# A convolution and GRU network on one core: first-image statistics on 128 partitions, matrices in long rows, a work tile less

## The chip, the cores and the metric

The kernel runs on one core of a Trainium2 chip. The metric is the device time of one execution, in microseconds (us). The median of three timed runs of the kernel before is 5883.06 us, the lowest 5861.34 and the highest 5891.94. One more execution was profiled; its own time is 5869.95 us.

## The reference, cut to what matters

The input x is (4, 64, 256, 256) in float32: four images of 64 channels. Two residual layers follow each other, each ahead of a group norm over 32 groups of two channels.

```python
x = x + conv(gn(x), w1, w_dw, w_out, ln_w, ln_b)
x = x + gru(gn(x), w_ih, w_hh, b_ih, b_hh)
```

The first layer takes the 64 channels to 384 by w1, runs a 3x3 depthwise convolution, and splits the result into q, k and v. It convolves q and k circularly in patches of 8x8 (through their Fourier transforms), normalizes over the channels, multiplies by v, and projects back to 64 channels by w_out. The second layer runs a GRU over the 256 columns of the image, in which each pixel sees three neighbours of the column before.

The group norm needs the mean and variance of every pair of channels over a whole image before the first pixel of that image can be normalized.

## The kernel before

Images are stored with their columns first, as x[b, c, w, h]. The work has three stages.

**Set-up.** A depthwise convolution followed by a Fourier transform of a patch is one linear map of a 10x10 halo (100 numbers) per channel. TensorE builds these maps from the taps (tile bt) and the depthwise weights (wd), ScalarE copies them into the tile ts (100 partitions, 384 channels, 64 numbers), and three stores on GpSimd's queue (POOL) write ts to the DRAM tensor t_all, one each for q, k and v (lines 229 to 248). Meanwhile SP's queue loads the first image in eight tiles xc (lines 249 to 255), each of 128 partitions by 4096 numbers. Partitions 0 to 63 hold the 64 channels of 16 columns in the left half of the image, 64 to 127 those of 16 columns in the right half. So there are two loads per tile, each of 64 rows of 16 KB. VectorE takes the statistics with bn_stats (512 numbers at a time) and bn_aggr. `norm_of_pieces` then joins partitions with a matmul by avg2 and gives a scale and shift per partition, sc0. Three tiles xc are held (bufs=3). After the set-up its pools are closed, and the pools of the next stage, xp for the image tiles xq among them, take their place in SBUF. Then the GRU's weights are loaded on ScalarE's queue (lines 258 to 266).

**Convolution, 32 blocks.** A block n is 32 rows of an image, in 128 patches. The loop from line 624 runs, for each block:

- pointwise, three times (chunks 0, 1, 2), 16 units each: TensorE multiplies the halos in the four tiles xq by w1, and ScalarE or VectorE copies the result from PSUM to the tile h;
- transform: 16 matrices of 100x1024 numbers for q and k and eight for v (function values) are fetched from t_all by SP into the tiles t (bufs=4, fetched four ahead, lines 329 to 340), and TensorE multiplies h by them;
- circular, twice (a = 0 and 1): the four products of the transforms of q and k (functions products and inverse);
- layer_norm, spread over the block by the generator norm, and, within the next block, gate, project and the store of the result (finish, lines 608 to 617).

The PSUM ring has eight banks. Temporary tiles q, k, pr, y, xr and others share one pool of seven work tiles of 128x1024 numbers (wk, line 278). All instructions keep the program's order on their engine (class InOrder), so a DMA that waits for a tile holds up what stands behind it on the same queue.

While the blocks of image b run, the statistics of image b+1 are taken (lines 597 to 606): look loads a quarter of a piece, four columns for each half, in two DMAs on POOL's queue into a work tile; count runs two bn_stats over it. Four quarters make a piece and eight pieces an image, so 24 of the 32 blocks do this. The work tile seen0 is held through circular(n, 0), another, seen1, from there to circular(n, 1). At an image's end norm_of_pieces runs between the pointwise units.

**GRU, 256 columns.** It reads the stored x1 column by column. Its first pools follow at line 701.

In the profile nearly all instructions have line 157, the helper that keeps the order, so they are told apart by the names of their tiles.

Of the kernel before, what the change touches and what calls it, by code (L numbers as in the profile page):

```python
# [10 lines left out]
F32 = mybir.dt.float32  # L11
AF = mybir.ActivationFunctionType
ALU = mybir.AluOpType
# [6 lines left out]
P = 128  # L20
# [63 lines left out]
def norm_of_pieces(nc, st, t, psum, eps, sc):  # L84

    m_all, d, total, mean = t[:, 128:136], t[:, 136:144], t[:, 144:145], t[:, 145:146]
    nc.vector.tensor_copy(m_all, st[:, :, 0])
    nc.vector.tensor_reduce(total, m_all, mybir.AxisListType.X, ALU.add)  # L90
    yield
    pm = psum()
    nc.tensor.matmul(pm, lhsT=t[:, 0:P], rhs=total, start=True, stop=True)
    nc.vector.tensor_copy(mean, pm)
    nc.vector.tensor_tensor(d, m_all, mean.to_broadcast([P, 8]), ALU.subtract)
    nc.vector.tensor_tensor(d, d, d, ALU.mult)
    nc.vector.tensor_tensor(d, d, st[:, :, 1], ALU.add)
    nc.vector.tensor_reduce(total, d, mybir.AxisListType.X, ALU.add)
    yield
    pv = psum()  # L100
    nc.tensor.matmul(pv, lhsT=t[:, 0:P], rhs=total, start=True, stop=True)
    nc.scalar.activation(sc[:, 1:2], pv, AF.Sqrt, bias=eps, scale=1.0)
    nc.vector.reciprocal(sc[:, 1:2], sc[:, 1:2])
    nc.vector.scalar_tensor_tensor(sc[:, 0:1], mean, -1.0, sc[:, 1:2], ALU.mult, ALU.mult)
    yield
# [57 lines left out]
def tile_conv_then_gru(  # L163
# [13 lines left out]
    bias: bass.AP,  # L177
    avg2: bass.AP,
    out: bass.AP,
):  # L180
# [6 lines left out]

    t_all = dram.tile([3, 8, HALO, 16 * NS], F32, tag="t_all", name="t_all")


    ident = const.tile([P, P], F32, tag="ident", name="ident")
    make_identity(tc.nc, ident)
    hh_sb = const.tile([P, P], F32, tag="hh", name="hh_sb")
    nc.scalar.dma_start(hh_sb, hh)
    eps = const.tile([P, 1], F32, tag="eps", name="eps")
    nc.gpsimd.memset(eps, EPS)
    w1_sb = const.tile([P, HID], F32, tag="w1", name="w1_sb")
    nc.scalar.dma_start(w1_sb, w1.rearrange("a c o -> (a c) o"))
    g_sb = const.tile([P, 2, 2, NS], F32, tag="g", name="g_sb")
    nc.scalar.dma_start(g_sb, g12.rearrange("a s r n p -> (a s) r n p"))  # L200
    wo_sb = const.tile([P, 2, C], F32, tag="wo", name="wo_sb")
    nc.scalar.dma_start(wo_sb, w_out.rearrange("a f t c -> (a f) t c"))
    ln_sb = const.tile([P, 2, 2], F32, tag="ln", name="ln_sb")
    nc.scalar.dma_start(ln_sb, ln.rearrange("a f n t -> (a f) n t"))

    def piece(of, b, i, w, n):

        for half in range(2):
            w0 = half * (W // 2) + i * (W // 16) + w
            yield slice(half * C, (half + 1) * C), of[b, :, w0 : w0 + n, :].rearrange("c w h -> c (w h)")  # L210

# [4 lines left out]
    bn0 = const.tile([P, 8, 6], F32, tag="bn0", name="bn0")  # L216
    with tc.tile_pool(name="xa", bufs=3) as xa, tc.tile_pool(name="sta", bufs=1) as sta, tc.tile_pool(
        name="bps", bufs=1, space=PSUM
    ) as bps:
        bt = sta.tile([P, 32, HALO], F32, tag="bt", name="bt")  # L220
        wd = sta.tile([P, HID], F32, tag="wd", name="wd")
        for i in range(4):
            nc.scalar.dma_start(bt[32 * i : 32 * i + 9], taps[i])
            nc.sync.dma_start(wd[32 * i : 32 * i + 9], w_dw)
        avg4 = sta.tile([P, 1024], F32, tag="avg4", name="avg4_0")
        nc.sync.dma_start(avg4[:, 0:P], avg2)
        ts = sta.tile([HALO, 3 * P, NS], F32, tag="ts", name="ts")
        banks = bps.tile([P, 8, 512], F32, tag="b", name="psb")
        for i in range(32):
            kind, s = i // 16, i % 16  # L230
# [12 lines left out]
            nc.scalar.copy(ts[:, c0 : c0 + num, 4 * s : 4 * s + 4], ps.rearrange("p s c -> p c s"))  # L243
        for i in range(3):
            nc.gpsimd.dma_start(
                t_all[i].rearrange("n p k -> p n k"),
                ts[:, i * P : (i + 1) * P].rearrange("p (n c) k -> p n (c k)", n=8),
            )
        for i in range(8):
            xc = xa.tile([P, 4096], F32, tag="xc", name=f"xc_{i}")  # L250
            for at, of in piece(x, 0, i, 0, 16):
                nc.sync.dma_start(xc[at], of)
            for k in range(8):
                nc.vector.bn_stats(bn0[:, k, :], xc[:, 512 * k : 512 * k + 512])
            nc.vector.bn_aggr(st0[:, i, :], bn0)
        for _ in norm_of_pieces(nc, st0, avg4, lambda: banks[:, 0, 0:1], eps, sc0[:, 0]):
            pass
    wi = const.tile([P, 9, C], F32, tag="wi", name="wi")
    wh = const.tile([P, 3, C], F32, tag="wh", name="wh")
    for a in range(2):  # L260
        at = slice(a * C, (a + 1) * C)
        for g in range(3):
            nc.scalar.dma_start(wi[at, 3 * g : 3 * g + 3, :], w_ih[g].rearrange("t c o -> c t o"))
            nc.scalar.dma_start(wh[at, g, :], w_hh[g])
    bias_sb = const.tile([P, 6], F32, tag="bias", name="bias_sb")
    nc.scalar.dma_start(bias_sb, bias.rearrange("a o n -> (a o) n"))
    b_rz = const.tile([P, 2], F32, tag="b_rz", name="b_rz")
# [3 lines left out]


    st1 = const.tile([P, NBLK, 2], F32, tag="st1", name="st1")
    with ExitStack() as s:
        big = s.enter_context(tc.tile_pool(name="big", bufs=1))
        xp = s.enter_context(tc.tile_pool(name="xp", bufs=4))
        tp = s.enter_context(tc.tile_pool(name="tp", bufs=4))
# [11 lines left out]
        def work(name, shape=(P, 1024)):  # L289
            return wk.tile(list(shape), F32, tag="wk", name=name)  # L290
# [3 lines left out]
        v = big.tile([P, NP, NS], F32, tag="v", name="v")  # L294
        xq = {}

        def load(n, jq):

            t = xp.tile([P, 16, HALO], F32, tag="xq", name=f"xq_{n}_{jq}")
            nc.gpsimd.dma_start(t, xh[n, :, 16 * jq : 16 * jq + 16, :])  # L300
            xq[n, jq] = t

        def normalize(n, jq):
# [25 lines left out]
        def fetch(count):  # L329
            while len(streamed) < min(count, NBLK * 24):  # L330
                m, r = divmod(len(streamed), 24)
                t = tp.tile([P, 16, NS], F32, tag="t", name=f"t_{m}_{r}")
                nc.sync.dma_start(t[0:HALO].rearrange("p c k -> p (c k)"), t_all[order[r][0], order[r][1]])
                streamed.append(t)
                matrices[m, order[r]] = t
# [122 lines left out]
        def layer_norm(n):  # L458

            st = big.tile([P, 2, NP // 2, 6], F32, tag="lnst", name=f"lnst_{n}")  # L460

# [134 lines left out]

        def look(n, k, t):

            for at, of in piece(x, n // 8 + 1, n % 8, 4 * k, 4):
                nc.gpsimd.dma_start(t[at], of)  # L600

        def count(n, k, t):
            for i in range(2):
                nc.vector.bn_stats(bn0[:, 2 * k + i, :], t[:, 512 * i : 512 * i + 512])
            if k == 3:
                nc.vector.bn_aggr(st0[:, n % 8, :], bn0)

# [11 lines left out]
        for jq in range(4):  # L619
            load(0, jq)  # L620
        for jq in range(4):
            normalize(0, jq)
        norm = None
        for n in range(NBLK + 1):
# [4 lines left out]
            if n == NBLK:  # L629
                for _ in norm:  # L630
                    pass
            if n:
                finish(n - 1)
            if n == NBLK:
                flush()
                later.pop()()
                break
            more = n // 8 + 1 < B
            if more:
                seen = work(f"seen0_{n}")  # L640
                look(n, 0, seen)
            circular(n, 0, lambda sp: count(n, 0, seen) if more and sp == 1 else None)
            if more:
                seen = work(f"seen1_{n}")
                look(n, 1, seen)
            for unit in range(16):
                pointwise(n, 1, unit, unit in (5, 8, 11, 14))
                if more and unit in (8, 14):
                    count(n, unit // 7, seen)
                    look(n, unit // 7 + 1, seen)  # L650
            flush()
            norm = layer_norm(n)

            def beside(sp):
                next(norm)
                if more and sp == 1:
                    count(n, 3, seen)

            circular(n, 1, beside)
            image = None  # L660
            if more and n % 8 == 7:
                t = work(f"avg4_{n}")
                nc.gpsimd.dma_start(t[:, 0:P], avg2)
                image = norm_of_pieces(nc, st0, t, lambda: psum()[:, 0, 0:1], eps, sc0[:, n // 8 + 1])
            for unit in range(16):
# [261 lines left out]
```

## Time and profile before

| what | value |
|---|---|
| median of three runs | 5883.06 us |
| the profiled execution | 5869.95 us |
| its span | 5868.2 us |
| TensorE (PE) busy | 5479.9 us, 93% |
| VectorE (DVE) busy | 4080.5 us, 70% |
| ScalarE (ACT) busy | 3475.4 us, 59% |
| GpSimd (POOL) busy | 500.8 us, 9% |
| moved by DMA | 818.04 MB, 139 GB/s on average |

The page cuts the span into 40 slices and gives each engine's busy share of a slice in tenths. It then follows the chain of work that ended last, lists the costliest groups of instructions with the idle time ahead of them, and the DMA queues: q0 holds the DMAs that POOL issues, q1 those of SP, q10 those of ScalarE. Other views give the instructions in order of time, the waits of an engine with what ended them, and the queues in any stretch. A busy TensorE is modelled from the records, and some records of matmuls may be missing.

### The profile page before, as it was taken

To read this page: it belongs to the slowest core of one execution; us is meant where nothing else is said; L and a number is where in the kernel's file an instruction comes from. 1 tells how busy PE (TensorE), PEld (TensorE's weight loads), DVE (VectorE), ACT (ScalarE), POOL (GpSimd) and SP (SyncE) were. 2 spreads that over 40 slices of the span, in tenths; PEclk is the share of its full clock that TensorE was granted. 3 is DMA by queue.
4 is the path that set the end of the run, shared out by engine and by line. 5 is a ranking of instruction groups with operands and counts; after the bars stand their busy time and mean duration, and the time that the engine had idled before them with its cause. 6 is when DMAs were issued, how large, how long until landed. Compare 5 with 4: busy or idle time off the path is not lost. (4 is left out here: it accounts for less than half of the span.)

```text
span 5868.2 us, 278629 instructions
## 1 busy us (share of the span) xinstructions
PE 5479.9 (93%) x127196; PEld 4762.6 (81%) x127196; DVE 4080.5 (70%) x9593; ACT 3475.4 (59%) x4604; POOL 500.8 (9%) x797
## 2 busy tenths in 40 slices
PE   2999999999999999999999999999979999999998
PEld 1878888888788878887888888878868888888888
DVE  2776777777767777777677767766667777776766
ACT  2556566665565656655655666556556666666655
POOL 0000000000000000000000000000002122222222
PEclk9999999999999999999999999999989999999999
DMA  8455555555555555555555454544444444444443
GB/s 225 135 156 147 151 151 155 154 142 152 157 147 154 150 151 159 141 150 159 150 152 150 140 143 126 142 139 125 137 114 116 116 116 117 115 117 113 116 114 81
DMA packets 561916, 818.04 MB, mean 139 GB/s; under 512 B 41353, under 2 KB 435373, under 8 KB 559677
## 3 DMA queue, kind: packets, MB, share of 16 engines
q1 hardware_dynamic: 520152, 633.59, 40.0%
q0 software_dynamic: 37776, 165.24, 9.5%
q8 instruction: 996, 16.32, 1.2%
q10 hardware_dynamic: 2808, 1.38, 0.1%
q14 instruction: 184, 1.50, 0.1%
HBM read 622.46 MB, written 144.05 MB: 131 GB/s over the span
## 5 line engine op out<-in xcount | busy, mean ns | idle before, releaser
L157 PEld LDWEIGHTS psring<-h,t 100*32 100x32 f32 x40960 | 1334.1, 115 | 294.0 <-issue 175.2
L157 PE MATMUL psring<-h,t 100*32 100x128 f32 x40960 | 1445.2, 274 | 105.9 <-issue 37.7
L157 PE MATMUL psring<-w_sb,xq 64*100 64x128 f32 x24576 | 1403.2, 271 | 55.7 <-POOL xq L157 40.2
L157 PEld LDWEIGHTS psring<-w_sb,xq 64*100 64x100 f32 x24576 | 1357.6, 164 | 117.0 <-issue 50.2
L157 ACT COPY h<-psring 100x1024 f32<-100x1024 f32 x1274 | 1205.5, 1027 | 161.4 <-PE psring L157 155.2
L157 DVE TENSOR_TENSOR pr<-psring,q 128x512 f32<-128x512 f32 (+1 forms) x576 | 463.3, 857 | 308.8 <-PE psring L157 234.8
L157 DVE BATCH_NORM_STATS2 lnst<-z 128x6 f32<-128x64 f32 x4096 | 545.4, 214 | 117.6 <-ACT z L157 117.6
L157 DVE TENSOR_TENSOR z<-z,lnm 128x1024 f32<-128x1024 f32 x512 | 612.7, 1218 | 8.8
L157 ACT COPY q<-psring 128x1024 f32<-128x1024 f32 x256 | 259.3, 1013 | 596.8 <-PE psring L157 358.9
L157 ACT ACTIVATE z<-pshz,b_rz 128x288 f32<-128x288 f32 (+7 forms) x510 | 242.6, 476 | 519.8 <-PE pshz L157 519.7
L157 PE MATMUL pshr<-st,wi 64*64 64x144 f32 (+7 forms) x12240 | 510.5, 270 | 34.9 <-issue 20.9
L157 PE MATMUL psni<-st,wi 64*64 64x144 f32 (+7 forms) x12240 | 510.4, 270 | 24.4 <-issue 22.4
L157 PE MATMUL pshz<-st,wi 64*64 64x144 f32 (+7 forms) x12240 | 510.8, 270 | 23.1 <-issue 21.9
L157 ACT COPY z<-psring 128x2048 f32<-128x2048 f32 x128 | 238.9, 1867 | 446.7 <-PE psring L157 441.7
L157 PE MATMUL psring<-pr,g_sb 32*64 32x512 f32 x8192 | 494.8, 594 | 5.7 <-issue 5.5
L157 ACT ACTIVATE y<-psring,ln_sb 128x512 f32<-128x512 f32 x512 | 372.5, 781 | 200.5 <-PE psring L157 197.0
L157 PEld LDWEIGHTS psni<-st,wi 64*64 64x64 f32 x12240 | 446.5, 133 | 45.5 <-issue 34.4
L157 PEld LDWEIGHTS pshr<-st,wi 64*64 64x64 f32 x12240 | 422.3, 133 | 52.3 <-issue 49.5
L157 DVE COPY h<-psring 100x1024 f32<-100x1024 f32 x262 | 320.3, 1223 | 198.7 <-PE psring L157 194.7
L157 PEld LDWEIGHTS pshz<-st,wi 64*64 64x64 f32 x12240 | 424.9, 133 | 37.3 <-issue 36.4
L157 DVE SCALAR_TENSOR_TENSOR g<-z,xn 128x288 f32<-128x288 f32 (+7 forms) x510 | 218.4, 428 | 311.9 <-ACT z L157 310.0
L157 POOL TENSOR_TENSOR raw<-raw,st 128x512 f32<-128x512 f32 x256 | 303.7, 1186 | 1146.0 <-ACT xn L157 548.1
(98 smaller groups left out, 7377.9 us busy)
## 6 DMA issues: line engine op xcount, KB each, us to landing
t<-t_all SPq DMA_DIRECT2D x768, 400.0 KB
xq<-in_xh POOLq DMA_DIRECT2D x128, 800.0 KB, 4.6
xr<-in_x SPq DMA_DIRECT2D x256, 256.0 KB
x<-xr SPq DMA_DIRECT2D x256, 256.0 KB
seen<-in_x POOLq DMA_DIRECT2D x192, 256.0 KB, 4.1
raw<-x SPq DMA_DIRECT2D x128, 256.0 KB
raw<-x SPq DMA_DIRECT2D x256, 128.0 KB
xt<-xn SPq DMA_DIRECT2D x256, 128.0 KB
```

The costliest lines, as they stand in the source:

```text
L157: return self.tc.keep_in_program_order(got(*args, **kwargs))
```

## The change

The change has six parts.

1. The first image's pieces have other partitions. Partition 2c + a holds channel c in half a of the image, for `(c a)` is one axis of equal steps in memory. So a piece is one DMA over 128 partitions. A tile xc is now half a piece (eight columns, rows of 8 KB), and five are held instead of three, 16 in all.
2. `norm_of_pieces` goes with it. The means of both layouts are needed (one to take from the statistics, one for the scale of xq, whose partitions are a C + c), so there are two small matrices, `sums`, and two matmuls for the mean.
3. The pool xp is opened ahead of the set-up's pools. The four loads of xq for block 0 are issued on POOL right behind the three stores of ts.
4. t_all is laid out as [3, 100, 8, 1024] instead of [3, 8, 100, 1024]. A store of one partition of ts is 32 KB in one run. A matrix is then read as 100 rows of 4 KB whose starts are 32 KB apart. The first two stores are issued after the first half of the copies.
5. The constants and the GRU's weights move to SP, between the sixth and seventh xc. The taps and wd come first on ScalarE's queue.
6. The statistics of other images use the tile lnst of the layer norm, while the layer norm doesn't, as a place for two columns at a time, and one work tile for four columns at a time. Each DMA spans 128 partitions. seen0 is gone: in circular(n, 0) no work tile is held for statistics.

```diff
 def norm_of_pieces(nc, st, t, psum, eps, sc):
...
-    nc.tensor.matmul(pm, lhsT=t[:, 0:P], rhs=total, start=True, stop=True)
+    for i in range(2):
+        nc.tensor.matmul(pm[:, i : i + 1], lhsT=t[:, P * i : P * i + P], rhs=total, start=True, stop=True)
...
-    t_all = dram.tile([3, 8, HALO, 16 * NS], F32, tag="t_all", name="t_all")
+    t_all = dram.tile([3, HALO, 8, 16 * NS], F32, tag="t_all", name="t_all")
+    layer0 = ExitStack()
+    xp = layer0.enter_context(tc.tile_pool(name="xp", bufs=4))
...
     def piece(of, b, i, w, n):
-        for half in range(2):
-            w0 = half * (W // 2) + i * (W // 16) + w
-            yield slice(half * C, (half + 1) * C), of[b, :, w0 : w0 + n, :].rearrange("c w h -> c (w h)")
+        w0 = i * (W // 16) + w
+        return of[b].rearrange("c (a w) h -> (c a) w h", a=2)[:, w0 : w0 + n, :].rearrange("p w h -> p (w h)")
...
         for i in range(4):
+            nc.scalar.dma_start(wd[32 * i : 32 * i + 9], w_dw)
             nc.scalar.dma_start(bt[32 * i : 32 * i + 9], taps[i])
-            nc.sync.dma_start(wd[32 * i : 32 * i + 9], w_dw)
...
+        def keep_matrices(i):
+            nc.gpsimd.dma_start(
+                t_all[i].rearrange("p n k -> p (n k)"),
+                ts[:, i * P : (i + 1) * P].rearrange("p c k -> p (c k)"),
+            )
...
-        for i in range(3):
-            nc.gpsimd.dma_start(
-                t_all[i].rearrange("n p k -> p n k"),
-                ts[:, i * P : (i + 1) * P].rearrange("p (n c) k -> p n (c k)", n=8),
-            )
-        for i in range(8):
-            xc = xa.tile([P, 4096], F32, tag="xc", name=f"xc_{i}")
-            for at, of in piece(x, 0, i, 0, 16):
-                nc.sync.dma_start(xc[at], of)
-            for k in range(8):
-                nc.vector.bn_stats(bn0[:, k, :], xc[:, 512 * k : 512 * k + 512])
-            nc.vector.bn_aggr(st0[:, i, :], bn0)
+            if i == 15:
+                keep_matrices(0)
+                keep_matrices(1)
+        keep_matrices(2)
+        for jq in range(4):
+            load(0, jq)
+        def seen_piece(i):
+            xc = xa.tile([P, 2048], F32, tag="xc", name=f"xc_{i}")
+            nc.sync.dma_start(xc, piece(x, 0, i // 2, i % 2 * 8, 8))
+            for k in range(4):
+                nc.vector.bn_stats(bn0[:, i % 2 * 4 + k, :], xc[:, 512 * k : 512 * k + 512])
+            if i % 2:
+                nc.vector.bn_aggr(st0[:, i // 2, :], bn0)
+        for i in range(6):
+            seen_piece(i)
...
+        for i in range(6, 16):
+            seen_piece(i)
...
-                nc.sync.dma_start(t[0:HALO].rearrange("p c k -> p (c k)"), t_all[order[r][0], order[r][1]])
+                nc.sync.dma_start(t[0:HALO].rearrange("p c k -> p (c k)"), t_all[order[r][0], :, order[r][1]])
...
+        seen = lnst.rearrange("p a i k -> p (a i k)")[:, 0:512]
-        def look(n, k, t):
-            for at, of in piece(x, n // 8 + 1, n % 8, 4 * k, 4):
-                nc.gpsimd.dma_start(t[at], of)
+        def look(n, w, t):
+            nc.gpsimd.dma_start(t, piece(x, n // 8 + 1, n % 8, w, t.shape[1] // H))
...
+            def beside_first(sp):
+                if more and sp in (0, 3):
+                    count(n, 2 * (sp // 3), seen)
+                    look(n, 2 * (sp // 3) + 2, seen)
+            circular(n, 0, beside_first)
             if more:
-                seen = work(f"seen0_{n}")
-                look(n, 0, seen)
-            circular(n, 0, lambda sp: count(n, 0, seen) if more and sp == 1 else None)
-            if more:
-                seen = work(f"seen1_{n}")
-                look(n, 1, seen)
+                four = work(f"seen_{n}")
+                look(n, 8, four)
             for unit in range(16):
                 pointwise(n, 1, unit, unit in (5, 8, 11, 14))
-                if more and unit in (8, 14):
-                    count(n, unit // 7, seen)
-                    look(n, unit // 7 + 1, seen)
+                if more and unit == 8:
+                    count(n, 4, seen)
+                    look(n, 6, seen)
+                    count(n, 8, four)
+                    look(n, 12, four)
+            if more:
+                count(n, 6, seen)
```

In place of the first `...` after `seen_piece(i)` the loads of sums, hh, w1, g, w_out, ln, w_ih, w_hh and the biases stand on SP. The first look of a block, `look(n, 0, seen)`, stands ahead of finish(n - 1). The last count, `count(n, 12, four)` with the bn_aggr, stays at sp == 1 of circular(n, 1).

## The prediction

> **What bounds the kernel now.** I read the 40 slices first. Each is 147 us long.
>
> ```profile
> PE   2999999999999999999999999999979999999998
> DMA  8455555555555555555555454544444444444443
> GB/s 225 135 156 147 151 151 155 154 142 152 157 147 154 150 151 159 141 150 159 150 152 150 140 143 126 142 139 125 137 114 116 116 116 117 115 117 113 116 114 81
> ```
>
> TensorE is full in every slice but the first, where it is busy for two tenths and the DMA engines for eight. So the kernel is bound by TensorE, except in a start-up of about one slice, and that start-up is bound by transfers. Next the timeline of the first 160 us. Its columns are start, duration, engine, line, operation, what it writes and reads, and in brackets the idle time before it and what ended that.
>
> ```profile
> 44.58 2.25 POOL L157 DMA_DIRECT2D t_all<-ts  x2 [43.22 <-ACT ts L157]
> ...
> 92.19 4.85 DVE L157 BATCH_NORM_STATS2 bn<-xc 128x6 f32<-128x512 f32 x8 [4.77 <-DMA xc<-in_x]
> ...
> 102.01 0.16 DVE L157 SCALAR_TENSOR_TENSOR sc<-avg,sc 128x1 f32<-128x1 f32 x1
> ...
> 126.77 6.07 SPq L157 DMA_DIRECT2D t<-t_all  x4
> 127.57 2.17 POOL L157 DMA_DIRECT2D xq<-in_xh  x4 [70.28 <-DMA t<-t_all]
> ...
> 136.08 1.72 ACT L157 ACTIVATE xq<-xq,sc 128x1600 f32<-128x1600 f32 x1 [34.30 <-DMA xq<-in_xh]
> ...
> 138.31 6.03 PEld L157 LDWEIGHTS psring<-w_sb,xq 64*100 64x100 f32 x64 [38.26 <-POOL xq L157]
> ...
> 147.00 1.11 DVE L157 TENSOR_SCALAR xq<-xq,sc 128x1600 f32<-128x1600 f32 x1 [13.89 <-DMA xq<-in_xh]
> ```
>
> The reader is to see a chain with idle time in it. The image's scale is ready at 102.01, yet the first image tile xq is only requested at 127.57. It waits for the matrices to land in t_all (126.77), because its pool lies where the set-up tiles were. The last of the four xq lands at 147.0, and the first pointwise stage ends at 161.3. The wait that ends last is t_all's landing, then xq's own 19.4 us.
>
> Third, the DMA queues in stretches of the start-up (packets, MB, share of 16 engines). From 28 to 42 us the loads xc are alone:
>
> ```profile
> q1 hardware_dynamic: 232, 3.01, 100.5%
> ```
>
> From 60 to 80 us xc (q1) and the stores to t_all (q0) share the engines:
>
> ```profile
> q1 hardware_dynamic: 320, 4.18, 82.8%
> q0 software_dynamic: 323, 0.82, 18.4%
> ```
>
> From 103 to 126 us t_all is the only large transfer:
>
> ```profile
> q0 software_dynamic: 1311, 3.77, 51.3%
> ```
>
> Alone, xc fills all engines and moves only 3.01 MB / 14 us = 215 GB/s, which is 13.4 GB/s per busy engine. Beside it the stores crawl at 0.82 / 20 us = 41 GB/s. Each xc row is 16 KB long and each t_all row 4 KB, so a fair turn per row would give about this split. Per busy engine, t_all does 3.77 MB / (0.513 x 16 x 23 us) = 20.0 GB/s. The xq loads, which span 128 partitions, do 20.6 late in the run (3500 to 4200 us: 17.07 MB at 7.4%). So what is slow is xc, in 64-partition halves, and what it starves.
>
> **The change, part by part.**
>
> *Start-up transfers.* Bytes hardly change. Before the last xq has landed the changed kernel moves 16.8 MB of xc, 9.8 MB of t_all, 3.3 MB of xq and about 1.5 MB of weights, taps and small matrices: 31.4 MB. I sum them as engine time at the rates above. xc in 128-partition pieces is not in this trace. Its ends are 13.4 GB/s per engine (nothing gained, 78 us) and the peak that the engines show when t_all drains (some 365 GB/s over the first 3 us from 90 us on, 46 us). I take 20.5, the rate of xq, its nearest row (128 partitions, 6.4 KB rows): 16.8 MB / (16 x 20.5) = 51 us. t_all at 20 GB/s per engine is 31 us. But its 100 rows don't load the engines evenly: by itself it took from about 85 us, with some 8.1 MB left, to 126.8, which is 194 GB/s or 51 us for all of it. Other loads now fill the gaps, so I take 36. xq at 20.6 is 10 us, the small ones 5, and the first request is out at 2.5 us. Sum: 2.5 + 51 + 36 + 10 + 5 = 104 us for the last xq, against 147.0. That is **43 us**.
>
> This needs the engines busy throughout. xq now has a pool of its own and is queued on POOL straight behind t_all, so no landing is waited for between them. The taps are issued first on ACT's queue instead of fifth to ninth (the last was issued at 12.8 us and its products began at 24.9), so t_all's first two stores should come at about 34 us instead of 44.6. By then VectorE isn't the limit: 64 statistics at 4.85/8 = 0.61 us are 39 us in all, 2.6 us per MB-piece, and the pieces come every 3.2 us. Five buffers of 1 MB cover its lag.
>
> What is late next: xq waits in the queue behind all of t_all, and the h tile lies on the set-up's tiles, so the first eviction still waits for t_all. Should the long t_all rows now take most turns from xc, the scale comes last instead of xq; the bytes are the same, the scale's own chain (97.1 to 102.0, 4.9 us) comes on top, and xq no longer trickles in. I keep both within the same number.
>
> *Weights.* Thirteen issues on ACT between 100.3 and 127.7 go. They lay beside t_all's landing and cost nothing; nor does their going give anything by itself. On SP, nine loads now stand between the sixth and the seventh xc. Each is under 0.3 MB; they are in the 5 us. If one had to wait for a tap load's landing, five pieces are already in flight to cover it.
>
> *One more matmul per image scale* (two columns for the mean): four images, 0.3 us each. 1 us.
>
> *Other images' statistics.* The order on TensorE and ScalarE stays; VectorE keeps its eight statistics per block in other places. The first layer-norm product of blocks 0, 24 and 31 starts at 238.47, 3371.24 and 4278.97. Blocks with statistics take 3132.8/24 = 130.53 us, those without 907.7/7 = 129.68. All the looking-ahead costs 0.85 x 24 = 20 us. Three image ends of 3 us each (the scale's chain, which stays) leave 11 us. In them are waits that show in VectorE's list from 160 to 3360 us (total, times, longest):
>
> ```profile
> DVE pr L157 <- DMA x<-xr: 68.4, 23, 3.8
> DVE bn L157 <- DMA seen<-in_x: 22.2, 24, 2.1
> ```
>
> From 3500 to 4300 us, without statistics, neither appears. The first is a shortage of work tiles in the first circular stage, where one tile less is now held; the second a load requested six units ahead of its use, now seven. VectorE's waits are mostly hidden behind TensorE, so of 11 us I take 4 as won. The ends are 11 won and 10 lost (each block adds a VectorE statistic ahead of the last projection; 0.4 us of it uncovered in 24 blocks).
>
> *Matrices in long rows.* Stores get longer runs; each matrix load now reads 100 rows of 4 KB that lie 32 KB apart, no longer one block. Not in this trace. Lower end: nothing, as the GRU's raw loads run well with 1 KB rows 256 KB apart (4600 to 5700 us: 122.2 MB at 40.2% of 16 engines, 17.3 GB/s each). Upper end below, as the rival. I take 0.
>
> The sum: 43 - 1 + 4 = 46 us. Against the profiled execution (5869.95 us, span 5868.2 and 1.75 around it) that is 5824. The median of the three timed runs, 5883, is 13 us above that execution, and the lowest 9 below it, so I put the forecast at **5826 us**.
>
> **Where a rule speaks against it.** xc halves show 215 GB/s with rows that start 256 KB apart; the new pieces start 128 KB apart. The Trainium skill ("DMA: Bandwidth & Descriptors", Latency and other measured facts) lists a row pitch of large powers of two as slow, 207 GB/s at 512 KiB. By it xc might stay at 207 GB/s: 81 us instead of 51, and 30 of the 46 us would go. Its page "SBUF — State Buffer" (The DMA port swizzle) gives the other reading: 64 partitions reach half of the 16 ports, at most 218 GB/s. By that one xc would be freed, at up to 436 GB/s, and the sum would be some 60 us. The raw loads above, at 17.3 per engine with the same 256 KB pitch, side with the ports, but not in a sustained stream.
>
> **The rivals.**
> *Slow rows stay slow (0.15).* xc keeps 13.4 GB/s per engine. Then xc ends near 88 us, t_all drains as before to about 124, and only the request and the gap between t_all and xq go: last xq 10 us later at 134, 13 us won instead of 43, so 5856. For it: this trace has no sustained stream of rows so far apart that is fast. Against: xq and raw.
> *Engines at their peak (0.15).* 31.4 MB at 365 GB/s is 86 us, last xq at 89, 58 us won: 5811.
> *Slower: matrix loads by far rows (0.05).* In the values stage TensorE takes a matrix of 0.41 MB each 1.86 to 1.97 us (two in the 3.71 us at 238.89), with four fetched ahead. That needs 210 to 220 GB/s. If far rows fall to half the 20 GB/s per engine, a matrix takes 2.56 us, 0.65 too long for the four not fetched ahead: 2.6 us per block, 83 in 32 blocks, so 5826 + 83 = 5909. It outweighs the gain from 46/32 = 1.4 us per block on, that is when a matrix takes over 2.27 us (180 GB/s). Against: the rows keep their 4 KB, and today TensorE waits for matrices only 9.6 us in all of 160 to 3360 us.
> *It does not do what it says:* xq might still wait for t_all through its pool; but its pool is now opened before the set-up's, so I give that nothing of its own.
>
> **How the numbers follow.** The forecast (40 to 50 us won) has 0.65, the rivals 0.15, 0.15 and 0.05. A measurement of this kernel can tell 0.5%, 29 us. Faster by more: forecast and peak, less 0.03 for noise, 0.77. Within: slow rows and that noise, 0.18. Slower by more: 0.05. The range runs from the peak with all 11 us of the steady part and from the lowest of the three runs (5811 - 7 - 9 = 5795) to the slow rows with 6 us of the possible loss in the blocks (5862).
>
> **What would show it.** A first slice with more TensorE, first pointwise at 92 to 100 us; xc alone at 300 GB/s or more; t_all landed before 100 us; the block period with statistics near 130.3; TensorE's wait for t unchanged. The forecast is wrong if xc alone stays near 215 GB/s, if t_all or the scale lands after 115 us, or if the period of the last blocks rises.

## The result, and the profile after

Five runs of the changed kernel have a median of 5838.45 us (5813.94 to 5845.49), five of the kernel before 5875.22 (5861.34 to 5891.94). The ratio is 0.9919, with a 95% interval of 0.9898 to 0.9939: about 48 us won, between 36 and 60. The profiled execution's span is 5836.7 us, 31.5 below that of before. A second group of runs gave 0.9904 [0.9880, 0.9928].

The forecast was 46 us won, at 5826 us; both stand close to this. The views must say whether it came the way that was told. First the 40 slices of the changed kernel:

```profile
PE   4999999999999999999999999999979999999998
DMA  7555555555555555555555554544444444444443
```

TensorE has four tenths of the first slice where it had two; the other slices are as they were. Then its timeline of the first 130 us (start, duration, engine, line, operation, what it writes and reads, count, and in brackets the idle time ahead and what ended it):

```profile
11.99 0.28 ACTq L158 DMA_DIRECT2D bt<-in_taps  x1
...
28.46 0.43 SPq L158 DMA_DIRECT2D bias_sb<-in_bias  x1
28.99 23.44 SPq L158 DMA_DIRECT2D xc<-in_x  x10
...
40.51 1.28 POOL L158 DMA_DIRECT2D t_all<-ts  x2 [39.17 <-ACT ts L158]
...
95.31 2.47 DVE L158 BATCH_NORM_STATS2 bn<-xc 128x6 f32<-128x512 f32 x4 [1.92 <-DMA xc<-in_x]
...
103.26 0.16 DVE L158 SCALAR_TENSOR_TENSOR sc<-avg,sc 128x1 f32<-128x1 f32 x1
...
103.55 26.03 SPq L158 DMA_DIRECT2D t<-t_all  x7
...
105.68 16.74 PE L158 MATMUL psring<-w_sb,xq 64*100 64x128 f32 x256 [4.30 <-POOL xq L158]
```

The first pointwise stage begins at 105.7 instead of 138.3, and its 256 matmuls now run in one piece to 122.4 instead of 161.3. But what came last has changed. In the trace t_all's last row ends at 86.1 us, where it ended at 125.4 before, and xq's last at 98.8. The scale is ready only at 103.26, no earlier than before: the last xc piece was counted at 97.8. The first read of t_all, at 103.55, had not waited for t_all either but for the scale, for its tile takes the place of set-up tiles. SP's list of waits from 0 to 110 us (total, times, longest) has it:

```profile
SPq L158 <- DVE sc L158: 43.2, 1, 43.2
```

The queues in three stretches show why the scale is late (packets, MB, share of 16 engines). From 35 to 40 us, xc alone:

```profile
q1 hardware_dynamic: 287, 2.10, 99.9%
```

That is 2.10 MB / 5 us = 420 GB/s, 26 per engine. From 5 to 20 us, xc beside the taps (q10):

```profile
q1 hardware_dynamic: 417, 3.04, 86.1%
q10 hardware_dynamic: 125, 0.50, 16.1%
```

The engines are as full, yet xc moves only 203 GB/s. From 60 to 78 us, xc beside the stores to t_all (q0):

```profile
q0 software_dynamic: 238, 5.32, 76.7%
q1 hardware_dynamic: 191, 1.40, 18.4%
```

Now it is xc that starves, at 78 GB/s, beside 296 on POOL's queue (275 of t_all, 21 of xq, which starts there at 57.8). The rows are 8 KB against mostly 32 KB, and the bytes stand at 1 to 3.8. Counted in rows, 171 stand against 209: again about one row of each in turn.

By position, in us of the two traces:

| | before | after | won |
|---|---|---|---|
| end of the first pointwise stage | 161.3 | 122.4 | 38.9 |
| first layer-norm product, block 0 | 238.5 | 202.2 | 36.3 |
| the 24 blocks with statistics | 3132.8 | 3139.6 | -6.8 |
| the 7 blocks without | 907.7 | 906.6 | 1.1 |
| the rest | 1589.2 | 1588.3 | 0.9 |

So the start-up holds the gain of the profiled execution. Whether the 24 blocks gained or lost can't be read from one pair of traces, as the experiments show.

### The profile page after: what moved, and what is told of

Same layout as the page of the kernel before. It is cut to its first block, busy times and chain, and to the rows that moved or that the text cites. A ratio compares the mean times of both kernels' runs of the same rounds, so it can differ in the third digit from the quotient of the medians.

```text
span 5836.7 us, 278467 instructions
## 1 busy us (share of the span) xinstructions
PE 5472.7 (94%) x127204; PEld 4752.8 (81%) x127204; DVE 4076.5 (70%) x9593; ACT 3475.0 (60%) x4604; POOL 476.3 (8%) x749
## 5 line engine op out<-in xcount | busy, mean ns | idle before, releaser
L158 DVE TENSOR_TENSOR y<-psring,y 128x1024 f32<-128x1024 f32 x256 | 312.4, 1221 | 128.8 <-ACT y L158 127.9
```

The lines of the kernel that those rows point to most:

```text
L158: return self.tc.keep_in_program_order(got(*args, **kwargs))
```

## The experiments

All kernels below compute the whole reference. Groups of runs differ in absolute time (the kernel before has medians from 5850 to 5915 us), so each is given as a ratio to the kernel before in its own group, and places in the start-up are read from its trace.

**The first image in halves again.** The theory: what freed xc is that one load spans 128 partitions. The rival: the shorter rows, or their smaller distance. Only the loads are halved; row length and distance stay.

```
-            nc.sync.dma_start(xc, piece(x, 0, i // 2, i % 2 * 8, 8))
+            for g in range(2):
+                at = slice(g * C, (g + 1) * C)
+                nc.sync.dma_start(xc[at], piece(x, 0, i // 2, i % 2 * 8, 8)[at])
```

> The changed kernel, but each piece xc of the first image comes in two loads, of partitions 0 to 63 and 64 to 127; rows of 8 KB and their distance of 128 KB stay. Theory (a load over half the partitions is slow, over all of them fast): xc alone falls from 420 GB/s (35 to 40 us of the changed kernel) to about 215, the scale is ready 25 to 35 us later than at 103.4, first pointwise at 128 to 140 instead of 105.7, and the time rises by 20 to 32 us. Rival (the shorter rows, or their smaller distance, made xc fast): xc alone stays above 380 GB/s and the time is within 6 us of the changed kernel.

Measured: 0.9959 [0.9945, 0.9973], so about half of the gain is gone. Its queues from 20 to 28 us, and its timeline:

```profile
q1 hardware_dynamic: 222, 1.44, 94.9%
q10 hardware_dynamic: 18, 0.12, 8.2%
```

```profile
131.82 0.16 DVE L158 SCALAR_TENSOR_TENSOR sc<-avg,sc 128x1 f32<-128x1 f32 x1
...
134.25 16.12 PE L158 MATMUL psring<-w_sb,xq 64*100 64x128 f32 x256 [4.30 <-POOL xq L158]
```

The engines are full and xc moves 1.44 MB / 8 us = 180 GB/s beside the last of the taps, and 1.65 MB / 8 us = 206 from 42 to 50 us without them; the scale comes 28.6 us later than in the changed kernel, and the first pointwise stage starts where the theory had it. The rival falls: the rows are the same. This settles the two readings weighed in the prediction. The Trainium skill ("SBUF — State Buffer", The DMA port swizzle and "Can I just issue two DMAs to hit both halves?") says that 64 partitions reach half of the ports, and that two transfers are not joined to fill them. Here both halves were requested one behind the other, and stayed slow. The pitch of 128 KB, in both kernels, cost the 128-partition loads nothing that shows: 420 GB/s.

**t_all in short rows again.** The theory: the 32 KB rows win their turns from xc and make the scale last.

```
-    t_all = dram.tile([3, HALO, 8, 16 * NS], F32, tag="t_all", name="t_all")
+    t_all = dram.tile([3, 8, HALO, 16 * NS], F32, tag="t_all", name="t_all")
```

(Store and fetch follow the old layout.)

> The changed kernel with the matrices stored as before: t_all is [3, 8, 100, 1024] again, rows of 4 KB. Theory (the two queues take turns row by row, so the 32 KB rows held xc back to 72 to 85 GB/s while t_all moved 264 to 333; the bytes are the bound): xc gets 200 GB/s or more beside t_all, the scale is ready at 80 to 92 us instead of 103.4, t_all lands later than 80 and xq last, first pointwise at 92 to 103 instead of 105.7; the time is 2 to 12 us lower. Rival (the long rows are what made the stores fast): t_all lands after 110, first pointwise after 115, the time rises by 8 us or more. The blocks without statistics keep 129.5 us in both.

Measured: 0.9921 [0.9898, 0.9943]. Its queues from 46 to 54 us and from 66 to 90, and its timeline:

```profile
q1 hardware_dynamic: 354, 2.57, 76.6%
q0 software_dynamic: 358, 0.77, 24.7%
...
q0 software_dynamic: 2361, 6.17, 93.6%
```

```profile
71.41 0.16 DVE L158 SCALAR_TENSOR_TENSOR sc<-avg,sc 128x1 f32<-128x1 f32 x1
...
104.79 1.47 SPq L158 DMA_DIRECT2D t<-t_all  x4
...
109.02 5.84 PE L158 MATMUL psring<-w_sb,xq 64*100 64x128 f32 x64 [39.48 <-POOL xq L158]
```

The turns change sides with the rows: 321 GB/s for xc, 96 for t_all. The scale is ready 32 us sooner, but this buys nothing: t_all's last row ends at 104.4 instead of 86.1, and xq trickles in until 117.0. Both expectations failed in part. From 66 to 90 us POOL's queue has the engines to itself and moves 257 GB/s, 224 of it t_all in 4 KB rows and the rest the first of xq. The long rows are worth 8.4 us in the start-up (first layer-norm product at 210.6 against 202.2, or 11.3 against the 199.3 of a second trace of the changed kernel), which the timed ratio doesn't resolve. In the blocks they do nothing either way: the 7 late blocks take 903.4 us here and 906.6 there, and TensorE's wait for t is 15.8 us in both from 160 to 3360 us.

**The other images' statistics as before**, in an otherwise changed kernel: old looks in halves, two work tiles.

```
-            circular(n, 0, beside_first)
+                seen = work(f"seen0_{n}")
+                look(n, 0, seen)
+            circular(n, 0, lambda sp: count(n, 0, seen) if more and sp == 1 else None)
...
+                seen = work(f"seen1_{n}")
+                look(n, 1, seen)
```

> The changed kernel with the statistics of the other images as before: halves of 64 partitions, two work tiles, four looks per block, and the old one-matmul scale for images 1 to 3. Theory (the new looks are worth nothing measurable): blocks with statistics take 130.5 to 130.9 us as in both kernels, the time is within 8 us of the changed kernel. Rival 1, as forecast (the new looks save 4 us): it is 2 to 11 us slower than the changed kernel, and the waits of VectorE for the store of xr and for seen return (68 and 22 us). Rival 2 (the new looks cost the 0.28 us per block that the two traces show): 5 to 10 us faster.

**Only the first image in 128-partition pieces**, in an otherwise unchanged kernel.

```
-        for i in range(8):
-            xc = xa.tile([P, 4096], F32, tag="xc", name=f"xc_{i}")
-            for at, of in piece(x, 0, i, 0, 16):
-                nc.sync.dma_start(xc[at], of)
...
+        for i in range(16):
+            xc = xa.tile([P, 2048], F32, tag="xc", name=f"xc_{i}")
+            w0 = i * (W // 32)
+            nc.sync.dma_start(
+                xc,
+                x[0]
+                .rearrange("c (a w) h -> (c a) w h", a=2)[:, w0 : w0 + 8, :]
...
```

> The kernel before with one part of the change alone: the first image in 16 pieces over 128 partitions (five tiles, two small matrices for its scale). Theory (pieces and early xq each carry a part): xc is through by 55 to 65 us, t_all then drains at 200 to 270 GB/s and lands at 92 to 105 instead of 126.8, the first xq is requested there, first pointwise at 104 to 117 instead of 138.3; 20 to 34 us faster than before. Rival (the gain came from the early request of xq): t_all lands after 115 and the gain is under 12 us.

**Only the early request of xq**, in an otherwise unchanged kernel: its pool is opened ahead of the set-up's, and the four loads stand behind the stores.

```
+    xp = layer0.enter_context(tc.tile_pool(name="xp", bufs=4))
...
+        for jq in range(4):
+            load(0, jq)
         for i in range(8):
```

> The kernel before with another part alone: the pool xp opened ahead of the set-up, the four xq of block 0 queued behind the stores to t_all; halves of 16 KB rows, matrices of 4 KB rows, the old statistics. Theory (the pieces carry most, the early request the rest): the stores still land near 124 to 128 us, the last xq at 130 to 138 instead of 147, first layer-norm product at 222 to 232 instead of 238.5; 8 to 16 us faster than before. Rival (the early request carries most): first layer-norm product before 215.

**Only the new looks**, in an otherwise unchanged kernel.

```
-                seen = work(f"seen0_{n}")
-                look(n, 0, seen)
...
+            circular(n, 0, beside_first)
...
+                four = work(f"seen_{n}")
+                look(n, 8, four)
```

> The kernel before with the third part alone: the other images' statistics through lnst and one work tile, over 128 partitions. The start-up stays (first layer-norm product at 238 us). Block time of the 24 blocks with statistics so far: new looks 3139.6, 3133.7, 3127.3, 3141.6 and 3127.6 us, old looks 3132.8, 3149.6, 3140.9 and 3132.1, means 3134 and 3139. Theory (worth 4 us, as forecast, below what a run can tell): 3126 to 3142 us, ratio to the kernel before 0.998 to 1.0005. Rival 1 (worth 15 us or more, which the timed medians of the run with the old looks suggest): ratio below 0.9975. Rival 2 (a cost): above 1.0005.

Measured, with the changed kernel's two groups for comparison:

| | ratio [95%] | scale ready | first pointwise stage | first layer-norm product | 24 blocks |
|---|---|---|---|---|---|
| changed kernel | 0.9919 [0.9898, 0.9939] | 103.3 | 105.7 to 122.4 | 202.2 | 3139.6 |
| changed kernel again | 0.9904 [0.9880, 0.9928] | 102.9 | 105.4 to 121.9 | 199.3 | 3141.6 |
| old looks | 0.9952 [0.9937, 0.9967] | 104.1 | 106.5 to 123.0 | 203.8 | 3149.6 |
| only the pieces | 0.9936 [0.9911, 0.9961] | 68.1 | 117.2 to 134.0 | 211.7 | 3140.9 |
| only early xq | 0.9982 [0.9966, 0.9998] | 101.0 | 139.2 to 157.8 | 234.9 | 3132.1 |
| only the new looks | 0.9981 [0.9967, 0.9994] | 101.2 | 142.6 to 165.2 | 241.8 | 3125.8 |

The pieces are the bulk: 26.8 of the 36.3 us in the start-up. Their first pointwise stage came just later than expected, since t_all landed only at about 105. The early request by itself wins 3.6 there, less than its expectation had: with slow halves, t_all still lands at 131.0 and xq at 143.3. Those 3.6 us are hardly more than what two traces of one kernel differ by (202.2 and 199.3), and the timed ratio leaves 1 to 20 us. The new looks alone win 0.0019 x 5850 = 11 us (4 to 19). Their rival of a cost falls; that of 15 us or more (below 0.9975) does not, for the interval reaches 0.9967. Taken out of the changed kernel they cost 0.0033 to 0.0048, 19 to 28 us, though across groups. That is over each range in that run's expectation, though the intervals of the two kernels just meet (0.9937 and 0.9939 at their ends); what it got right is that the two waits of VectorE return. In its trace the 7 blocks without statistics are slower too (917.7 us, 906.6 and 904.6 in the changed kernel), so not all of the difference need be the looks. VectorE's list of waits shows which went. Old looks in the changed kernel, 160 to 3360 us (total, times, longest):

```profile
DVE pr L182 <- DMA x<-xr: 60.6, 24, 3.6
DVE bn L182 <- DMA seen<-in_x: 24.0, 25, 2.0
```

The new looks in the changed kernel:

```profile
DVE pr L158 <- DMA x<-xr: 6.9, 14, 0.9
DVE bn L158 <- DMA seen<-in_x: 0.3, 1, 0.3
```

The shortage of work tiles is gone, and with it ScalarE's wait for pr (205.2 us in 41 times with the old looks, 14.0 in 7 with the new). If 191 us fewer of it are worth some 11, most of it must have lain beside TensorE's work; no run tries that by itself. The sums over 24 blocks can't settle so small a gain: kernels with new looks have 3122 to 3150 us (3160 with the 16 KB rows below), with old ones 3132 to 3150.

**The taps in 128 partitions.** Theory: the nine-partition tap loads halve xc in the first 20 us, and SP then stands at small matrices until 28.46. So the taps come padded in one load each, and the constants stand behind the 13th piece.

```
-            nc.scalar.dma_start(wd[32 * i : 32 * i + 9], w_dw)
-            nc.scalar.dma_start(bt[32 * i : 32 * i + 9], taps[i])
+        nc.scalar.dma_start(wd, w_dw)
+        nc.scalar.dma_start(bt, taps)
...
-        for i in range(6):
+        for i in range(13):
             seen_piece(i)
```

> The changed kernel, but the taps and the depthwise weights come in one load each over 128 partitions (23 rows of zeros behind each 9, 1.8 MB instead of 0.5), and the nine constants stand on SP behind the thirteenth piece xc instead of the sixth. Theory (the taps' loads over 9 partitions slow xc and, through the constants' turns on SP, hold back its issue, so xc gets 175 to 233 GB/s in the first 20 us): xc plus taps get 330 GB/s or more from 5 to 20 us, the first stores to t_all are issued at 24 to 30 instead of 40.5, first pointwise at 90 to 98 instead of 105.7, 6 to 14 us faster than the changed kernel. Rival (the start is bound by all the bytes at the rate they have): first pointwise at 104 or later, no gain.

Measured: 0.9923 [0.9903, 0.9943]; scale at 101.7, first pointwise at 104.1, not at 90 to 98. Its DMA from 15 to 30 us, and SP's timeline:

```profile
q1 hardware_dynamic: 862, 6.28, 101.1%
```

```profile
31.44 0.43 SPq L158 DMA_DIRECT2D avg<-in_sums  x1
...
72.30 0.33 SPq L158 DMA_DIRECT2D bias_sb<-in_bias  x1
77.47 5.13 SPq L158 DMA_DIRECT2D xc<-in_x  x3
```

The theory held for the first 30 us (419 GB/s; the stores went out at 32 us, a little behind the 24 to 30 expected), and the gain was lost behind them: the constants, in rows of at most 2.3 KB, took their turns against 32 KB rows, SP needed 41 us to issue nine of them, and the last three pieces waited behind.

**The same, with even rows of 16 KB for both** (store and fetch follow the layout).

```
-    t_all = dram.tile([3, HALO, 8, 16 * NS], F32, tag="t_all", name="t_all")
+    t_all = dram.tile([3, 2, HALO, 4, 16 * NS], F32, tag="t_all", name="t_all")
...
+            xc = xa.tile([P, 4096], F32, tag="xc", name=f"xc_{i}")
...
```

> The kernel of the run with taps on 128 partitions, and rows of 16 KB on both queues: pieces xc of 16 columns (three tiles), t_all as [3, 2, 100, 4, 1024]. Theory (turns go row by row, so equal rows share evenly): beside t_all xc gets 130 to 210 GB/s, the scale is ready before the last xq has landed, at 70 to 88 us, and first pointwise starts with the first xq at 84 to 95; 0 to 8 us faster than that run. Rival (the stores need their 32 KB rows to be fast): t_all lands 8 us or more later than in that run and nothing is gained.

Measured: 0.9973 [0.9959, 0.9986]. From 60 to 80 us the two queues moved the same, 185 GB/s each, within the 130 to 210 expected:

```profile
q0 software_dynamic: 465, 3.70, 53.2%
q1 hardware_dynamic: 302, 3.69, 43.6%
```

So the even turns came, but not the gain. The constants held up the scale again (102.9): the last rows of the last two of them moved only at 61 and 70 us, behind t_all's. And t_all's last row ended at 96.4, where it ended at 74.7 in the run before, as the rival had it. The kernel lost most in the blocks: 3160.3 us for 24, with TensorE waiting for t for 34.5 us in 51 times. Why this layout does so was not tried further.

**The padded taps, constants behind the sixth piece** (the lines are set against the first kernel with padded taps).

```
-        for i in range(13):
+        for i in range(6):
             seen_piece(i)
```

> The kernel with taps on 128 partitions, but the nine constants back behind the sixth piece xc, ahead of the stores to t_all. In the run with them behind the thirteenth they were issued from 31.4 us and the next xc only at 77.5: theory, that each of their rows of 0.5 to 2.3 KB waits a turn of a 32 KB row. Then here the constants are through before the stores begin (32 us), the last xc is issued before 50, the scale is ready at 84 to 95 instead of 102 to 103, first pointwise at 86 to 97; 6 to 16 us faster than the changed kernel. Rival (some other wait held back the last three xc): the scale stays above 100.

Measured: 0.9914 [0.9898, 0.9930]; scale at 97.3, first pointwise 99.7 to 116.3, first layer-norm product 194.9. From 5 to 20 us:

```profile
q1 hardware_dynamic: 653, 4.69, 74.9%
q10 hardware_dynamic: 185, 1.68, 26.3%
```

6.37 MB / 15 us = 425 GB/s, where the changed kernel moved 236 at the same busy share. So the taps' loads over nine partitions did cost xc its rate; that they were eight loads and are now two changed with it, and wasn't tried apart. Theory and rival both fell: the scale came under 100, but not at 84 to 95. The better start is worth 4 to 7 us at the first layer-norm product, since t_all starves xc after that (94 GB/s from 40 to 60 us, beside 301).

**All large loads in one queue**, in the order xc, t_all, xq, so that nothing takes turns with xc; the constants alone on SP.

```
-            nc.sync.dma_start(xc, piece(x, 0, i // 2, i % 2 * 8, 8))
+            nc.gpsimd.dma_start(xc, piece(x, 0, i // 2, i % 2 * 8, 8))
...
+        for i in range(3):
+            keep_matrices(i)
+        for jq in range(4):
+            load(0, jq)
```

> As the run with the constants behind the sixth piece and taps on 128 partitions, but the pieces xc are issued on POOL, and the three stores to t_all and the four xq behind them on the same queue, so that no turns are shared. Theory (the turns against the 32 KB rows hold xc and with it the scale back; the bytes at 350 to 420 GB/s are the floor): the last piece is counted before 60 us, the scale ready at 52 to 66, t_all lands at 76 to 88, first pointwise starts with the first xq at 80 to 92; 12 to 24 us faster than the changed kernel, first layer-norm product at 178 to 190. Rival (stores or xq alone in the queue are slower than mixed, so the sum stays): first pointwise at 98 or later.

**The same with xq ahead of the stores.**

```
-        for i in range(3):
-            keep_matrices(i)
         for jq in range(4):
             load(0, jq)
+        for i in range(3):
+            keep_matrices(i)
```

> The run with all large transfers of the start-up in POOL's queue, but with the four xq ahead of the three stores to t_all. There the scale was ready at 60.5 us, but the last xq landed at 97.9, beside the first reads of matrices, and the first pointwise stage took from 89.3 to 112.8. Theory (transfers go in the order of the queue; h waits for the stores, whose tile it overlays, but four of the 16 units fit in PSUM ahead of that): xq lands before 68 us, first pointwise starts at 62 to 72, stalls until the stores land at 84 to 92, and ends at 96 to 105 instead of 112.8; first layer-norm product at 178 to 188 instead of 194.2, 8 to 15 us faster than that run. Rival (what ends the start-up is the landing of t_all and the first matrices, whatever stands ahead): first pointwise ends later than 108 and the first layer-norm product comes after 190.

Measured: 0.9907 [0.9886, 0.9927] and 0.9906 [0.9890, 0.9923]. With one queue the scale is ready at 60.5, t_all lands at 84.5, and the first pointwise stage runs from 89.3 to 112.8 (TensorE's timeline):

```profile
89.35 6.43 PE L158 MATMUL psring<-w_sb,xq 64*100 64x128 f32 x64 [30.75 <-POOL xq L158]
...
100.84 11.93 PE L158 MATMUL psring<-w_sb,xq 64*100 64x128 f32 x176 [1.04 <-DVE h L158]
```

Scale, landing and start came as expected. But xq's last tiles come beside the first reads of t, so the first layer-norm product is at 194.2, not at 178 to 190. With xq first:

```profile
62.99 5.36 PE L158 MATMUL psring<-w_sb,xq 64*100 64x128 f32 x64 [4.30 <-POOL xq L158]
...
98.95 13.12 PE L158 MATMUL psring<-w_sb,xq 64*100 64x128 f32 x192 [30.60 <-issue]
```

TensorE begins at 63.0, does the 64 matmuls that need no eviction, and stalls until t_all has landed (97.6): the first eviction writes h, which lies on the set-up's tiles that the stores still read. The stores' tail is what remains: from 85 to 99 us they move only 1.15 MB, at 24.3% of the engines. First layer-norm product: 190.3, and the first pointwise stage ends at 112.1, so it is the rival that held. These versions bring that product 5 to 12 us forward of the changed kernel's two traces, at most 0.2% of the time, which their intervals don't separate from it; none is shown to beat it.

## Why the prediction was right, and where it was not

The mechanism stands: a start-up bound by transfers, freed by pieces that span 128 partitions and an early xq, with TensorE's blocks nearly untouched. That the forecast of 46 us came so close to 48 is in part luck, for its terms miss in both directions.

- *xc at 20.5 GB/s per engine* was mis-sized low: 26 alone, so 16.8 MB need 40 us at that rate, not 51. The rival of slow rows falls, by the halves kernel. (*"The raw loads above, at 17.3 per engine"* spoke for neither reading: those 122.2 MB are all of SP's queue there, stores and loads of 64 partitions among them.)
- *"They are in the 5 us"*, for the nine loads on SP, failed. Small loads cost turns, not bytes: the seventh xc was issued at 28.99, and the taps halved xc from 5 to 20 us. *"The taps are issued first, so t_all's first two stores should come at about 34"* failed with it: 40.5. The padded taps gave 32.
- The two misses about cancelled: the last xq packet came at 98.8, for 104 worked out.
- *"Should the long rows take most turns, the scale comes last ... I keep both within the same number."* It did come last, at 103.3, and the price was not nothing: the first pointwise stage started at 105.7, not at 92 to 100, and the start-up won 36 to 39 us, not 43.
- *t_all at 36 us*: its sign, the landing before 100, was met. The last row ended at 86.1, and in the one-queue kernel t_all's rows moved from 49.2 to 84.0, 35 us. The uneven tail behind the term shows as well: 1.15 MB in 14 us with xq first.
- *Looks, 4 of 11 us*: 11 alone, 4 to 19, so the upper bound was nearer. *One more matmul, 1 us* was not measured apart from this. With the 36 us that the start-up won in one trace, the looks' timed 11 make 47, beside 48 timed; with intervals this wide that is no proof.
- *Block period near 130.3*: 3139.6/24 = 130.8 in the trace, too small a difference for one trace to show, as said.
- *Long and far rows, 0*: failed for the start-up, where the long rows win 8 to 11 us, and held for the blocks (907.7 and 906.6). TensorE's wait for t, 9.6 us before and 15.8 after, is 15.8 with short rows and 6.5 to 18.8 in the others but the 16 KB one, so it isn't the far rows. The rival of far reads falls.
- The rival of engines at their peak fails through the turns and tails: 31.4 MB in the 96.3 us from 2.5 to 98.8 are 326 GB/s, not 365.

What stays open: what the looks win to within a few us, what the new order of the small loads (part 5) is worth by itself, which no run took out alone, and why 16 KB rows made TensorE wait for t.

## What to carry over

A sum of bytes over a rate tells when the engines are done, but not which transfer is last: look at the row lengths of everything that shares them, because the longest rows win, and at small loads ahead of large ones in an issuing queue. One queue for a stage's large loads, in an order that you choose, sets which of them comes last: here it brought the scale from 103.3 to 60.5 us, but the first layer-norm product only 5 to 12 us forward, since the bytes stayed. Speeding up one transfer of three in a start-up moves the end to the next: scale, then t_all, then xq each came last in some kernel here.

## What the runs showed of the hardware

- Engines that the profile shows as full can move half: xc moved 215 GB/s to 64 partitions and 420 to 128. Loads of 0.5 MB to nine partitions held a 128-partition load beside them to 203 GB/s; with the same taps over 128 partitions, in two loads instead of eight, both together moved 425.
- Two queues shared the engines more nearly row by row than in equal bytes. Rows of 16 KB against 4 KB split 209 to 41 GB/s, 8 against 32 (with some of 6.4) split 78 to 296, 8 against 4 split 321 to 96, and 16 against 16 split 185 to 185. In rows that is 255 to 200, 171 to 209, 314 to 189 and 225 to 256.
- The stores of 100 rows ran at 233 GB/s in rows of 4 KB (only the pieces, 62 to 80 us), and at 7.14 MB / 24 us = 298 in rows of 32 KB (xq first, 61 to 85 us), before a tail of 1.15 MB in 14 us at 24.3% of the engines. With the first of xq beside them, from 52 to 72 us of the one-queue kernel, the queue moved 7.22 MB / 20 us = 361 GB/s.
